# Long convolution of a decoder layer: blocks of 64 tokens on partition halves in place of blocks of 128

## Chip, cores and metric

The kernel runs on one core of a Trainium2 chip. The metric is device time in microseconds. Before the change three runs took 2181.34, 2184.97 and 2187.56 us; their median is 2184.97 us. All data are float32.

The engines are called PE (TensorE, matrix multiply), DVE (VectorE), ACT (ScalarE), POOL (GpSimd) and SP (SyncE, which here only issues transfers). A PE matmul needs a weight load ahead of it, shown as PEld.

## What is computed

A decoder layer on x of 16 sequences x 512 tokens x 256 channels: a gated long-convolution block, then self plus cross attention, then a low-rank feed-forward, each followed by a layer norm. The change touches the first part:

```python
z = rmsnorm(u, pre_norm_w) @ in_proj_w.T              # 768 channels
z_pre = conv1d(z, short_w, causal, 3 taps, per channel) + short_b
x2, x1, v = split(z_pre, 3)
h = sum_s residues[:, s] * exp(log_poles[:, s] * t)   # a filter of 512 taps per channel, 16 poles
xv = x1 * v
y = (causal_convolution(xv, h) + xv * D_skip) * x2
y = y @ out_proj_w.T + u                              # then an MLP
```

## The kernel before

**Two parts, each with its own plan.** The front (until about 326 us) works out the long convolution of all sequences; its results go to DRAM. The loop then takes one sequence after another through the gate, the MLP, attention and the feed-forward. In each part the operations are first collected (`plan.op`: engines, a cost, a function, a priority, what it reads and writes) and then ordered by the class `Plan` (lines 62 to 195): a list scheduler in which each engine takes the startable operation of lowest priority number. Each operation's tiles come from named pools and are bound in that planned order. Engines and transfer queues then work in that order, each waiting where its input is not there. `Plan.change` (line 96) adds a bonus to a PE operation that has the same array tiling as the one before, with the constants `HOLD` and `STAY`.

**Projection** (`project(b)`, line 422, once a sequence). x is loaded; `rms_ops` squares it on ACT; `rsqrt_op` works out the factor on POOL; `scale_ops` (line 325) scales the four row blocks of 128 x 256 on DVE (line 330); PE transposes (line 344); six matmul groups (line 456) give the 768 channels; ACT (line 463) and DVE (line 471) apply the three taps; POOL multiplies x1 by v (line 487); PE transposes the product (line 495), and it is kept as `xv`: 128 token positions on the partitions, and per channel 4 blocks x 16 sequences. The gate x2 goes to DRAM (line 481). Weights of the loop are loaded in between; POOL scales two of them (line 787).

**Long convolution** (lines 582 to 708), in blocks of 32 channels, eight in all. Time is cut into 4 blocks of 128 tokens:
- *toe*: within a block of tokens the filter is a 128x128 Toeplitz matrix per channel. It is read from `hpad` in DRAM with overlapping rows (`load_toe`, line 593: 8 channels, 512 KB, 32 loads in all); POOL clears the part beyond the diagonal (line 602); `toe_mm` (line 670) multiplies, two channels at once on the two column halves of the array.
- *near*: `near_mm` (line 619) reduces a block of tokens to 16 states per channel, four channels at once on column groups of 32; DVE moves the result out (line 629).
- *recurrence*: two steps per channel block carry the states from one token block to the next (POOL, lines 639 and 647), through one tile `tmp`.
- *far*: ACT evaluates exponentials (line 655); `far_mm` (line 683) adds the older blocks' share to toe's result in PSUM.
- ACT and DVE copy the sums to `row` tiles (line 694, by the helper at lines 297 and 299), and ACT issues the writes to `yconv` in DRAM (line 701, 64 of 128 KB).

**Hand-over to the loop.** SP issues the loads of `yt` from `yconv` (`load_y`, line 1002, two per sequence), of the gate (line 1008) and of x (line 1011); POOL multiplies y by the gate (line 1020); PE begins with the output projection (line 1033).

Before, `toes`, `far`, and the x tiles share the pool "x" of 11 tiles; the pool "row" has 9.

## Time and profile before

| What | Value |
|---|---|
| Median of three runs | 2184.97 us |
| Profiled execution | 2186.31 us, span 2184.6 us |
| Instructions in the span | 35354 |
| PE busy | 2037.0 us (93%) |
| DVE busy | 1361.0 us (62%) |
| ACT busy | 943.6 us (43%) |
| POOL busy | 663.5 us (30%) |
| Granted PE clock | 0.97 |
| Transfers | 177.94 MB, mean 81 GB/s |

The profile is one execution. In its groups a row gives line, engine, operation, output <- input by tile names (`fmm`, `mm` are PSUM tiles, `fx` a tile of the pool "x", `frow` one of "row"), shapes, count, and in the timeline the start and the length of the stretch; the bracket at its end gives the idle time before it and what ended that. "issue" means that the engine waited for nothing that the profile shows. In the names of array tiles, 128*64 is 128 rows by 64 columns.

The front's stages are seen by the lines that run in them: projection (line 456 on PE) from 11.4 to 228 us, near, toe and far (lines 619, 670, 683) from 229.0 to 308.5 us, and the first output projection (line 1033) at 326.4 us.

### The profile page before, as it was taken

The numbers are of one execution on the slowest core, as the hardware profiler recorded it, in microseconds if no ns is written. First come the engines' busy times: TensorE is split into PE (matmuls) and PEld (weight loads), VectorE is DVE, ScalarE is ACT, GpSimd is POOL, SyncE is SP. The second block draws the span as 40 slices with busy tenths as digits, with TensorE's granted clock in tenths as the row PEclk, the third lists the DMA queues.
The fourth block names the chain that finished last, engine by engine and source line by source line (L and its number), as shares of the span: only waits on it lengthen the run. The fifth ranks groups of instructions, "written<-read, shape, count | busy, mean of one in ns | idle before, by whom it ended". The sixth has DMA issues, their size and how long they took to land.

```text
span 2184.6 us, 35354 instructions
## 1 busy us (share of the span) xinstructions
PE 2037.0 (93%) x14324; PEld 1053.6 (48%) x14324; DVE 1361.0 (62%) x1988; ACT 943.6 (43%) x1385; POOL 663.5 (30%) x896
## 2 busy tenths in 40 slices
PE   8999758979899999999999999999999999999676
PEld 4444545535454545454545454545454545454332
DVE  7988311746565757575757575757575757575642
ACT  7765312142526262626262626262626262625243
POOL 3333451131323232324232424242424242323222
PEclk9999978989999999999999999999999999999888
DMA  5342582122222222222232313131313131212200
GB/s 176 123 133 83 198 270 73 49 63 66 70 59 89 59 88 61 83 66 86 62 91 57 94 55 93 56 94 55 95 54 96 52 87 52 68 51 68 61 11 10
DMA packets 113733, 177.94 MB, mean 81 GB/s; under 512 B 13217, under 2 KB 61858, under 8 KB 113442
## 3 DMA queue, kind: packets, MB, share of 16 engines
q1 hardware_dynamic: 108450, 167.29, 25.0%
q10 hardware_dynamic: 5120, 8.39, 1.2%
q8 instruction: 112, 1.84, 0.3%
q14 instruction: 51, 0.42, 0.1%
HBM read 109.00 MB, written 66.67 MB: 80 GB/s over the span
## 4 chain that ended last, share of the span: by engine, by line
PE 84%; ACT 5%; DVE 5%; DMA 3%; issue 2%; POOL 1%; ACTq 0%; SPq 0%; POOLq 0%; DVEq 0%
PE mm L1058 13%; PE scores L1302 10%; PE mm L1211 8%; PE mm L1110 7%; PE scores L1380 7%; PE av L1415 7%; PE fmm L456 6%; PE mm L1605 4%; PE av L1621 3%; PE mm L1139 3%; PE mm L972 2%; DMA fx<-hpad 2%; PE mm L344 2%; PE mm L1467 2%; ACT ex L1392 2%
## 5 line engine op out<-in xcount | busy, mean ns | idle before, releaser
L1392 ACT ACTIVATE ex<-scores 128x2048 f32<-128x2048 f32 x160 | 300.1, 1876 | 176.7 <-PE scores L1380 174.0
L1058 PE MATMUL mm<-xT,w_l 128*128 128x512 f32 x640 | 296.0, 606 | 0.0
L1403 POOL TENSOR_SCALAR_AFFINE_SELECT ex<-ex 128x512 f32<-128x512 f32 x256 | 158.0, 635 | 382.4 <-ACT ex L1392 351.1
L1302 PE MATMUL scores<-keys,q 32*128 32x320 f32 (+4 forms) x2560 | 233.8, 472 | 42.8 <-DVE maxes L1332 18.3
L1321 DVE TENSOR_TENSOR scores<-scores,mask_qk 128x512 f32<-128x512 f32 (+1 forms) x192 | 168.3, 876 | 101.9 <-PE scores L1302 97.9
L1302 PEld LDWEIGHTS scores<-keys,q 32*128 32x128 f32 x2560 | 116.5, 190 | 179.0 <-issue 57.8
L1613 ACT ACTIVATE row<-mm,b_s 128x512 f32<-128x512 f32 x128 | 80.8, 684 | 253.6 <-PE mm L1605 253.4
L1380 PE MATMUL scores<-q,keys 32*128 32x512 f32 (+3 forms) x2048 | 183.1, 460 | 7.1 <-ACT ex L1392 7.0
L1058 PEld LDWEIGHTS mm<-xT,w_l 128*128 128x128 f32 x640 | 115.6, 190 | 145.9 <-issue 128.6
L456 PE MATMUL fmm<-fx,inw 128*128 128x512 f32 x384 | 177.2, 607 | 2.2 <-ACT fx L299 2.2
L957 ACT ACTIVATE xt<-xt,small 128x256 f32<-128x256 f32 x192 | 102.7, 595 | 173.7 <-POOL small L950 173.7
L1549 POOL TENSOR_TENSOR nd<-nd,nd 128x1024 f32<-128x1024 f32 x30 | 70.6, 2354 | 347.3 <-DMA nd<-di 347.3
L1415 PE MATMUL av<-ex,va 128*32 128x512 f32 (+3 forms) x2048 | 168.1, 439 | 0.0
L306 POOL TENSOR_SCALAR small<-small 128x4 f32<-128x4 f32 (+1 forms) x66 | 13.1, 199 | 509.6 <-DVE small L942 508.1
L1070 ACT ACTIVATE row<-mm 128x512 f32<-128x512 f32 x80 | 47.8, 597 | 271.0 <-PE mm L1058 271.0
L297 DVE COPY row<-av 128x512 f32<-128x512 f32 x66 | 45.7, 692 | 184.0 <-PE av L1415 165.5
L1110 PE MATMUL mm<-w_l,gT 128*128 128x256 f32 x640 | 158.9, 384 | 0.0
L471 DVE SCALAR_TENSOR_TENSOR frow<-fmm,cw,frow 128x511 f32<-128x511 f32 x192 | 140.2, 745 | 14.5 <-ACT frow L463 10.5
L1334 DVE TENSOR_REDUCE maxes<-scores 128x4 f32<-128x2048 f32 x64 | 146.7, 2293 | 2.2
L1380 PEld LDWEIGHTS scores<-q,keys 32*128 32x128 f32 x2048 | 89.3, 183 | 104.4 <-ACT ex L1392 33.8
L1110 PEld LDWEIGHTS mm<-w_l,gT 128*128 128x128 f32 x640 | 117.9, 190 | 43.8 <-issue 30.3
L1217 DVE TENSOR_SCALAR q<-mm,bqc_s 128x512 f32<-128x512 f32 x63 | 47.3, 751 | 140.0 <-PE mm L1211 140.0
(177 smaller groups left out, 3322.8 us busy)
## 6 DMA issues: line engine op xcount, KB each, us to landing
dn<-row SPq DMA_DIRECT2D x120, 256.0 KB
fx<-hpad SPq DMA_DIRECT2D x32, 512.0 KB
keys<-dk SPq DMA_DIRECT2D x64, 256.0 KB
nd<-dn SPq DMA_DIRECT2D x30, 512.0 KB
nd<-di SPq DMA_DIRECT2D x30, 512.0 KB
fx<-in_x SPq DMA_DIRECT2D x16, 512.0 KB
gates<-frow SPq DMA_DIRECT2D x32, 256.0 KB
yconv<-frow ACTq DMA_DIRECT2D x64, 128.0 KB
```

Of the source, the lines that this page charges most:

```text
L456: nc.tensor.matmul(ps.t, inw[:, k, bass.ts(m, P)], xT.t[:, k, :], start=(k == 0), stop=(k == KD - 1))
L471: lambda e, m=m, lag=lag, ps=ps, t=t: nc.vector.scalar_tensor_tensor(t.t[:, lag:], ps.t[:, 0 : T - lag], cw[:, m, 2 - lag : 3 - lag], t.t[ ...
L1058: nc.tensor.matmul(ps.t, w[:, k, bass.ts(f, P)], zT.t[:, k, :], start=(k == 0), stop=(k == KD - 1))
L1110: nc.tensor.matmul(ps.t[:, bass.ts(cc, D)], gT.t[:, f, bass.ts(c, P)] if f < NF else gE.t, w_l3[:, f, :] if f < NF else w_l3e[:, c, :], st ...
L1211: nc.tensor.matmul(ps.t, w[:, k, cols], xT.t[:, k, :], start=(k == 0), stop=(k == KD - 1))
L1302: nc.tensor.matmul(sc.t[:, r, at : at + hi - lo], q.t[hd, bass.ts(i, P)], kk.t[hd, lo:hi], start=True, stop=True,)
L1321: nc.vector.tensor_tensor(diag, diag, mask, ALU.add)
L1334: nc.vector.tensor_reduce(own[:, 3], sc.t, AX.X, ALU.max, negate=True)
L1380: nc.tensor.matmul(sc.t[:, r, at : at + T - j * P], keys[g].t[hd, TC + j * P : TC + (j + 1) * P], qas[g].t[hd, j * P :], start=True, stop= ...
L1392: lambda e, sc=sc, ex=ex: nc.scalar.activation(ex.t.rearrange("p (r n) -> p r n", r=HPG), sc.t, AF.Exp, scale=scale),
L1403: lambda e, ex=ex, at=at: nc.gpsimd.affine_select(out=ex.t.rearrange("p (r n) -> p r n", r=HPG)[:, :, at : at + P], in_=ex.t.rearrange("p ...
L1415: nc.tensor.matmul(av[g].t[bass.ts(r, SLOT), j * P :], va.t[:, j, h * VS : h * VS + SLOT], ex.t[:, r * T + at : r * T + at + n], start=(j ...
```

## The change

The token blocks of the long convolution become 64 long, so there are eight instead of four. The two blocks of a pair lie on the two partition halves that they already have in `xv`.

- The Toeplitz matrices are 64x64. A load covers 16 channels and fills both partition halves with the same values by two transfers of 256 KB; there are 16 such tiles in place of 32. POOL clears them by a multiplication with a constant triangle `tri` instead of a select. `toe_mm` uses array tiles of 64x64, four at once.
- `near_mm` uses tiles of 64x32 and works out both halves separately, into two PSUM tiles; two evictions on DVE. `far_mm` runs per half, 64 columns each.
- The recurrence has six steps in place of two; a step (two instructions) may go to DVE or to POOL, as the planner chooses.
- `far` has a pool of its own (2 tiles); "x" has 10 tiles, "row" 8. The state tile is twice as wide.
- `yconv` gets a leading index for the half; `load_y` issues four loads per sequence in pieces of 256 bytes in place of two in pieces of 512.
- In the front, x is scaled on POOL; the projection matmuls are only planned once their `row` tile is free (`holds`); the planner's tiling bonus is 0 in the front and 1000 in the loop as before.

```diff
-    def __init__(self, tiles):
+    def __init__(self, tiles, hold=0, stay=0):
         self.tiles, self.ops = tiles, []
+        self.HOLD, self.STAY = hold, stay
...
-    HOLD, STAY = 1000, 1000
...
-    hpad = dram.tile([D + 1, P], F32, name="hpad")
-    yconv = dram.tile([NT, B, D, P], F32, name="yconv")
+    HB = P // 2
+    hpad = dram.tile([D + 1, HB], F32, name="hpad")
+    yconv = dram.tile([2, NT, B, D, HB], F32, name="yconv")
...
-    def scale_ops(x, sq, prio, on="DVE"):
+    def scale_ops(x, sq, prio, on):
         for c in range(NT):
             def fn(e, c=c):
-                if e == "DVE":
-                    nc.vector.tensor_scalar(x.t[:, c, :], x.t[:, c, :], sq.t[:, c, 8:9], None, ALU.mult)
+                if e == "POOL":
+                    nc.gpsimd.tensor_scalar(x.t[:, c, :], x.t[:, c, :], sq.t[:, c, 8:9], None, ALU.mult)
                 else:
                     nc.scalar.activation(x.t[:, c, :], x.t[:, c, :], AF.Copy, scale=sq.t[:, c, 8:9])
-            plan.op(on, 0.4 if on == "DVE" else act(D, True), fn, prio, r=[sq], w=[(x, c)])
+            plan.op(on, pool_(D) if on == "POOL" else act(D, True), fn, prio, r=[sq], w=[(x, c)])
...
-            "x": tiles(fp_, "fx", 11, [P, R8 * P]),
-            "row": tiles(fp_, "frow", 9, [P, T]),
-            "state": tiles(fp_, "state", 2, [P, R8, HPG * B]),
+            "x": tiles(fp_, "fx", 10, [P, R8 * P]),
+            "row": tiles(fp_, "frow", 8, [P, T]),
+            "state": tiles(fp_, "state", 2, [P, R8, 2 * NT * B]),
+            "far": tiles(fp_, "far", 2, [P, R8, HB]),
...
+        tri = fp_.tile([P, HB], F32, name="tri")
+        nc.gpsimd.memset(tri, 1.0)
+        for n in range(2):
+            half = bass.ts(n, HB)
+            nc.gpsimd.affine_select(
+                out=tri[half, :], in_=tri[half, :], compare_op=ALU.is_ge, fill=0.0, base=HB - 1,
+                pattern=[[-1, HB]], channel_multiplier=-1,
+            )
...
-            scale_ops(x_, sq, pr - 120)
+            scale_ops(x_, sq, pr - 120, "POOL")
...
-                plan.op("PE", KD * pe(T), mm, pr + 10, r=[xT, INW], w=[ps])
+                plan.op("PE", KD * pe(T), mm, pr + 10, r=[xT, INW], w=[ps], holds=[t])
...
-            for c in range(HPG):
-                toe = View("x", lambda t: t.rearrange("p (d u) -> p d u", u=P))
-                def load_toe(e, toe=toe, at=d0 + c * R8):
-                    hp = hpad[at : at + R8, :]
-                    src = bass.AP(hp.tensor, hp.offset, [[1, P], [1, R8 * P]])
-                    nc.sync.dma_start(out=toe.t.rearrange("p d u -> p (d u)"), in_=src)
-                early = blk * HPG + c < 5
+            for cp in range(HPG // 2):
+                toe = View("x", lambda t: t.rearrange("p (d u) -> p d u", u=HB))
+                def load_toe(e, toe=toe, at=d0 + cp * 2 * R8):
+                    hp = hpad[at : at + 2 * R8, :]
+                    for n in range(2):
+                        src = bass.AP(hp.tensor, hp.offset, [[1, HB], [1, 2 * R8 * HB]])
+                        nc.sync.dma_start(out=toe.t[bass.ts(n, HB)].rearrange("p d u -> p (d u)"), in_=src)
+                early = blk * HPG // 2 + cp < 5
                 plan.op(
-                    "SP", 0.4, load_toe, pc - 50, r=[HPAD], w=[toe], lat=4.0,
-                    after=at_seq(4 + c if early else B - 1),
+                    "SP", 1.0, load_toe, pc - 50, r=[HPAD], w=[toe], lat=4.0,
+                    after=at_seq(4 + 2 * (blk * HPG // 2 + cp) if early else B - 1),
                 )
                 plan.op(
-                    "POOL", 1.35,
-                    lambda e, toe=toe: nc.gpsimd.affine_select(
-                        out=toe.t, in_=toe.t, compare_op=ALU.is_ge, fill=0.0, base=P - 1,
-                        pattern=[[0, R8], [-1, P]], channel_multiplier=-1,
+                    "POOL", pool_(2 * R8 * HB),
+                    lambda e, toe=toe: nc.gpsimd.tensor_tensor(
+                        toe.t, toe.t, tri.unsqueeze(1).to_broadcast([P, 2 * R8, HB]), ALU.mult
                     ),
                     pc - 50, w=[toe],
                 )
                 toes.append(toe)
-            ps, st = Buf("mm"), Buf("state")
-            far = View("x", lambda t: t.rearrange("p (r u) -> p r u", u=P))
+            pss, st = [Buf("mm"), Buf("mm")], Buf("state")
+            far = Buf("far")
             for rr in range(0, R8, 2):
-                def near_mm(e, rr=rr, ps=ps, d0=d0):
+                def near_mm(e, rr=rr, pss=pss, d0=d0):
                     for r in range(rr, rr + 2):
                         for c in range(HPG):
                             d = d0 + c * R8 + r
-                            nc.tensor.matmul(
-                                ps.t[bass.ts(c, SLOT), bass.ts(r, (NT - 1) * B)],
-                                near[:, d * NS : d * NS + SLOT], xv[:, d, 0 : (NT - 1) * B],
-                                start=True, stop=True,
-                            )
-                plan.op("PE", 0.25, near_mm, pc, r=[XV, NEAR], w=[ps], tiling=COLS4)
-            def evac_state(e, ps=ps, st=st, blk=blk):
-                n = (NT - 1) * B
-                nc.vector.tensor_tensor(
-                    st.t[:, :, B:], ps.t[:, 0 : R8 * n].rearrange("p (r n) -> p r n", n=n),
-                    rsT[:, bass.ts(blk, R8)].unsqueeze(2).to_broadcast([P, R8, n]), ALU.mult,
-                )
-            plan.op("DVE", 0.6, evac_state, pc, r=[ps, (LP, "T1")], w=[st])
-            for j in range(2, NT):
+                            for n in range(2):
+                                half = bass.ts(n, HB)
+                                nc.tensor.matmul(
+                                    pss[n].t[bass.ts(c, SLOT), bass.ts(r, NT * B)],
+                                    near[half, d * NS : d * NS + SLOT], xv[half, d, :], start=True, stop=True,
+                                )
+                plan.op("PE", 0.45, near_mm, pc, r=[XV, NEAR], w=pss, tiling=BOTH, holds=[st])
+            for n in range(2):
+                def evac_state(e, n=n, ps=pss[n], st=st, blk=blk):
+                    cols = (NT - n) * B
+                    at = NT * B if n == 0 else B
+                    nc.vector.tensor_tensor(
+                        st.t[:, :, at : at + cols], ps.t.rearrange("p (r n) -> p r n", r=R8)[:, :, 0:cols],
+                        rsT[:, bass.ts(blk, R8)].unsqueeze(2).to_broadcast([P, R8, cols]), ALU.mult,
+                    )
+                plan.op("DVE", 0.7, evac_state, pc, r=[pss[n], (LP, "T1")], w=[(st, n)])
+            for j in range(2, 2 * NT):
+                before, at = ((j - 1) % 2 * NT + (j - 1) // 2) * B, (j % 2 * NT + j // 2) * B
+                def step(e, before=before, at=at, st=st, blk=blk, tmp=None):
+                    eng = nc.vector if e == "DVE" else nc.gpsimd
+                    eng.tensor_tensor(
+                        tmp.t, st.t[:, :, before : before + B],
+                        aT[:, bass.ts(blk, R8)].unsqueeze(2).to_broadcast([P, R8, B]), ALU.mult,
+                    )
+                    eng.tensor_tensor(st.t[:, :, at : at + B], st.t[:, :, at : at + B], tmp.t, ALU.add)
                 tmp = Buf("tmp")
                 plan.op(
-                    "POOL", 0.5,
-                    lambda e, j=j, tmp=tmp, st=st, blk=blk: nc.gpsimd.tensor_tensor(
-                        tmp.t, st.t[:, :, bass.ts(j - 1, B)],
-                        aT[:, bass.ts(blk, R8)].unsqueeze(2).to_broadcast([P, R8, B]), ALU.mult,
-                    ),
-                    pc, r=[st, (NEAR, "a")], w=[tmp],
-                )
-                plan.op(
-                    "POOL", 0.5,
-                    lambda e, j=j, tmp=tmp, st=st: nc.gpsimd.tensor_tensor(
-                        st.t[:, :, bass.ts(j, B)], st.t[:, :, bass.ts(j, B)], tmp.t, ALU.add
-                    ),
-                    pc, r=[tmp], w=[st],
+                    "DVE POOL", (0.6, 1.0), lambda e, step=step, tmp=tmp: step(e, tmp=tmp), pc,
+                    r=[(NEAR, "a")], w=[st, tmp],
                 )
             for r in range(R8):
...
+            for cp in range(HPG // 2):
+                def toe_mm(e, cp=cp, ys=ys, toe=toes[cp], d0=d0):
+                    for r in range(R8):
+                        for cc in range(2):
+                            c = 2 * cp + cc
+                            for n in range(2):
+                                half = bass.ts(n, HB)
+                                nc.tensor.matmul(
+                                    ys[c].t[bass.ts(n ^ cc, HB), bass.ts(r, HB)], xv[half, d0 + c * R8 + r, :],
+                                    toe.t[half, cc * R8 + r, :], start=(r == 0), stop=False,
+                                    skip_group_check=True,
+                                )
+                plan.op("PE", 1.2, toe_mm, pc + 10, r=[XV, toes[cp]], w=ys[2 * cp : 2 * cp + 2], tiling=(HB, HB))
+            for rr in range(0, R8, R8 // 2):
+                def far_mm(e, rr=rr, ys=ys, st=st, far=far):
+                    for r in range(rr, rr + R8 // 2):
+                        for n in range(2):
+                            for c in range(HPG):
+                                part = slice(c * SLOT, c * SLOT + NS)
+                                nc.tensor.matmul(
+                                    ys[c].t[bass.ts(n ^ c % 2, HB), bass.ts(r, HB)],
+                                    st.t[part, r, bass.ts(n, NT * B)], far.t[part, r, :],
+                                    start=False, stop=True, skip_group_check=True,
+                                )
+                plan.op("PE", 0.95, far_mm, pc + 10, r=[st, far], w=ys, tiling=(SLOT, P // 2))
             for c in range(HPG):
-                def toe_mm(e, c=c, ys=ys, toe=toes[c], d0=d0):
-                    for rp in range(R8 // 2):
-                        for par in range(2):
-                            r = par * R8 // 2 + rp
-                            nc.tensor.matmul(
-                                ys[c].t[bass.ts(par, 64), bass.ts(rp, P)], xv[:, d0 + c * R8 + r, :],
-                                toe.t[:, r, :], start=(rp == 0), stop=False, skip_group_check=True,
-                            )
-                plan.op("PE", 0.9, toe_mm, pc + 10, r=[XV, toes[c]], w=[ys[c]], tiling=COLS2)
-            for par in range(2):
-                def far_mm(e, par=par, ys=ys, st=st, far=far):
-                    for rp in range(R8 // 2):
-                        r = par * R8 // 2 + rp
-                        for c in range(HPG):
-                            part = slice(c * SLOT, c * SLOT + NS)
-                            nc.tensor.matmul(
-                                ys[c].t[bass.ts(par, 64), bass.ts(rp, P)], st.t[part, r, :], far.t[part, r, :],
-                                start=False, stop=True, skip_group_check=True,
-                            )
-                plan.op("PE", 0.65, far_mm, pc + 10, r=[st, far], w=ys, tiling=(SLOT, P // 2))
...
-                        lambda e, c=c, o=o, par=par, d0=d0: nc.scalar.dma_start(
-                            out=yconv.rearrange("j b d t -> (j b) d t")[
-                                :, d0 + c * R8 + par * R8 // 2 : d0 + c * R8 + (par + 1) * R8 // 2, :
+                        lambda e, c=c, o=o, n=n, d0=d0: nc.scalar.dma_start(
+                            out=yconv[n].rearrange("j b d t -> (j b) d t")[
+                                :, d0 + c * R8 : d0 + (c + 1) * R8, :
                             ],
-                            in_=o.t[bass.ts(par, 64)],
+                            in_=o.t[bass.ts(n ^ c % 2, HB)],
...
-    plan = Plan(pool)
+    plan = Plan(pool, 1000, 1000)
...
         def load_y(e, k):
-            nc.sync.dma_start(
-                out=yt.t[:, k, :].rearrange("p (j t) -> p j t", j=NT),
-                in_=yconv[:, b, bass.ts(k, P), :].rearrange("j p t -> p j t"),
-            )
+            for n in range(2):
+                nc.sync.dma_start(
+                    out=yt.t[:, k, :].rearrange("p (j n t) -> p j n t", n=2, t=HB)[:, :, n],
+                    in_=yconv[n, :, b, bass.ts(k, P), :].rearrange("j p t -> p j t"),
+                )
...
-            plan.op("SP", 0.1, lambda e, k=k: load_y(e, k), p0 - 500, w=[(yt, k)], lat=4.0)
+            plan.op("SP", 1.0, lambda e, k=k: load_y(e, k), p0 - 500, w=[(yt, k)], lat=4.0)
```

## The prediction

> **What bounds the kernel now.** I read the windows first, to find the stage that the change touches; then PE's timeline inside it, for what ends its waits; then the DMA queues; last the chain behind it. Columns of the windows: length, then busy time and count for PE, weight loads (PEld), DVE, ACT, POOL, then granted clock, DMA share, GB/s.
>
> ```profile
> core 0: us, PE busy (x) PEld busy (x) DVE busy (x) ACT busy (x) POOL busy (x), PEclk, DMA share, GB/s
> 200.00:220.00 20.00, 19.69 (x66) 10.02 (x65) 18.03 (x31) 11.54 (x15) 5.17 (x6) 1.00 0.25 64
> 240.00:260.00 20.00, 12.86 (x288) 11.34 (x286) 3.51 (x6) 6.65 (x21) 8.45 (x11) 0.95 0.73 255
> 280.00:300.00 20.00, 15.69 (x281) 14.18 (x279) 3.50 (x6) 2.34 (x4) 14.62 (x21) 0.79 0.92 352
> ...
> 1000.00:1200.00 200.00, 199.33 (x1410) 100.22 (x1408) 125.75 (x173) 89.74 (x114) 64.23 (x82) 1.00 0.27 81
> ```
>
> Up to 229 us (projection) PE is full. From 229.0 to 308.5 us (the convolution, 79.5 us) no engine is full, but the DMA engines are at 0.9: 27 of the 32 Toeplitz loads of 512 KB fall here. From about 400 us the loop keeps PE at 99.7%. In the built programs PE, DVE, ACT and POOL hold the same loop instructions in the same order before and after, so only the front (0 to 326 us) can move the time, if the loop's loads stay hidden.
>
> The Toeplitz load is halved, so the question is what bounds the convolution next. PE's timeline at its start, before the loads collect:
>
> ```profile
> 229.03 1.90 PE L619 MATMUL fmm<-xv,near 128*32 128x48 f32 x157
> 234.88 2.72 PE L619 MATMUL fmm<-xv,near 128*32 128x48 f32 x128 [3.95 <-issue]
> 238.60 1.30 PE L619 MATMUL fmm<-xv,near 128*32 128x48 f32 x99 [1.01 <-issue]
> 239.83 1.85 PE L670 MATMUL fmm<-fx,xv 128*64 128x128 f32 x29
> 242.61 2.18 PE L670 MATMUL fmm<-fx,xv 128*64 128x128 f32 x35 [0.92 <-issue]
> ```
>
> PE stops with nothing to wait for ("issue"), after 128 records, and again after 99 + 29 = 128. Each matmul record has a weight load beside it, so a stop comes every 256 instructions. The page says what that is:
>
> ```profile
> PE 2037.0 (93%) x14324; PEld 1053.6 (48%) x14324; DVE 1361.0 (62%) x1988; ACT 943.6 (43%) x1385; POOL 663.5 (30%) x896
> ...
> q8 instruction: 112, 1.84, 0.3%
> ```
>
> 2 x 14,324 instructions over 112 packets is 256 per packet, 1.84 MB / 112 = 16.4 KB: PE fetches its code in pages of 256 instructions, and small matmuls use up a page faster than the next arrives. The DMA view of 238 to 242 us, with one stop in it, has nothing else on the engines:
>
> ```profile
> DMA packets 1, 0.02 MB, mean 4 GB/s; under 512 B 0, under 2 KB 0, under 8 KB 0
> q8 instruction: 1, 0.02, 1.4%
> ```
>
> From page to page: 238.60 - 234.88 = 3.72 us, 242.61 - 238.60 = 4.01 us; mean **3.87 us**. In it the packet starts 1.0 to 1.6 us after the page begins (235.92, 240.15 us in the trace) and lasts 1.0; PE goes on some 1.6 us later. Under the full DMA of 248 to 303 us the packet starts 0.6 to 7.9 us after its page, mean 4.7.
>
> **The change, part by part.**
>
> *Convolution, PE.* near, toe and far each go from 256 to 512 matmuls. A float32 matmul leaves two records with two weight loads (512 records for 256 matmuls on L619, L670, L683). So 3 x 256 x 4 = 3,072 PE instructions become 6,144: 12 pages become 24. Streams alone shrink: toe runs at 55 ns a record (32 in 1.97 us, two tiles at once) and far at 22; halved columns on four or eight tiles should give some 14 and 11; with near at 11, 1,024 x (11 + 14 + 11) ns = 37 us, 1.4 to 1.8 us a page, far below 3.87. So pages set the pace. The 57 instructions to the next page boundary take 0.3 us; the first page lasts 5.5 us (229.33 to 234.88 before; its successor's packet was late behind Toeplitz and gate transfers, and such stand there again); then 22 pages at c, and 1.7 us of work in the last: 7.5 + 22c. For c the ends are 3.5 (the shortest such step in the convolution, 267.71 to 271.21) and 5.1. DMA work left is 6 loads x 128 packets x 180 ns and the yconv writes (1.2% of 16 engines' span, 419 engine-us): (138 + 419)/16 = 35 us of about 100, a share of 0.34; between 1.27 us of start delay at none and 4.7 at 0.9 a straight line gives 2.55, so c = 3.87 + 1.28 = 5.1. A queue grows slower than a line at first, so I take **c = 4.3**: 102.1 us. Against 79.5: **+22.6** (ends +5 and +40).
>
> [...]
>
> [...] The new toe_mm sends both row halves of a channel group into one bank. No row of before does this. Unhindered 14 ns a record; serial 53 (half of 107, twice the 55 above, for half the columns): 6.8 us a page, 2.5 over c on 8 pages, +20. I take nothing, since even two at once (27 ns, 3.4 us) stays under c; the 20 goes into the range.
>
> *Convolution, the rest, hidden under 3c = 12.9 us a block.* Two masks on POOL as multiply, 2.35 us each for 1,024 elements (L1549) instead of four selects of 1.09: 4.7. Six recurrence steps instead of two, serial through one tmp tile, 0.40 + 0.46 + 0.1 us each on POOL at most (L639, L647): 5.8. ACT: 8 DMA issues of 0.55, 2 copies of 0.58, 8 exponentials of 64 columns of 0.24 (L580): 7.5. DVE: two evictions of 0.6, two copies of 0.69, some steps: about 5. Late next if cover is gone: the last far, two pages (8.6 us) after the last near; its eviction and steps take 7.0. Nothing added.
>
> *Projection.* Scaling x moves to POOL. One 256-column row there: L787 takes 1.97 us for 672, L306 0.20 for 4, so 0.87 us; four 3.5 against 1.14 on DVE. The first sequence has no cover: **+2.4**. Later ones are a sequence ahead (13.4 us each; POOL then has 1.25 + 3.5 + 2.5 = 7.3). A gain is in reach here:
>
> ```profile
> 160.63 7.94 POOL L787 TENSOR_SCALAR w_l<-w_l,postw 128x672 f32<-128x672 f32 x4 [1.83 <-DMA postw<-in_post_w]
> ```
>
> ```profile
> 175.84 0.36 PE L344 MATMUL fmm<-ident,fx 128*128 128x128 f32 x1 [3.35 <-issue]
> 176.94 3.56 PE L344 MATMUL fmm<-ident,fx 128*128 128x128 f32 x15 [0.74 <-DVE fx L330]
> ```
>
> The weight scaling held up POOL's rsqrt, PE ran dry for 4.3 us and restarted at a clock of 0.80 to 0.86, some 2.5 more. In the changed order one x more is scaled ahead of it, and about 18 us of PE work cover its 13: **-7** (ends 0 and -10: all visible PE gaps of the projection are some 22 us, most with other causes). Fewer row tiles (8) and the hold on them: 0 to +6, taken 0; waits for rows now are under 5 us in all (ACT L463 behind DVE L471). Sum **-4.5**.
>
> *Hand-over.* Last far to first loop matmul now:
>
> ```profile
> 317.43 3.15 DMA yconv<-frow
> 320.64 0.37 SPq L1002
> 321.06 3.87 DMA gate<-gates
> 325.06 1.27 POOL yt L1020
> ```
>
> The last write is issued 9.5 us after the last far, as ACT still has a block of writes before it (6 us of issues and copies against 5.1 between the last two fars). With blocks 12.9 us apart only its own 6.2 remain: -3.3. One more load stands before the gate, 0.37, and 1,024 pieces of 256 B for 512 of 512 B, at most 30 ns each over 16 engines: +0.3 more likely than +1. **-2.6**. In the loop the two extra loads per sequence (0.7 us of SP in 107) lie beside a full PE: 0.
>
> *Sum*: -4.5 + 22.6 - 2.6 = +15.5. The profiled execution took 2186.3 (span 2184.6 and 1.7 around it), giving 2201.8; it lies 1.3 above the median 2185.0: **2201 us**.
>
> **Rivals.**
> (a) *Pages cost nothing in time*, and the halved transfers count. For: DMA is at 0.9 now, and many pages of the busy stretch passed with no stop. Against: those lasted 6 us and more. Then ACT is next: 8 x 7.5 + 7 lead-in = 67, -12.5; projection -4.5; ACT's backlog at the end stays: about 2169, faster. It decides if a page comes in under 2.5 us.
> (b) *Fetching at its quickest*, c = 3.5 to 3.7, and a projection gain near -8: +5 to +9, -8, -2.6, no change: 2182. For: 3.50 was seen under a loaded DMA.
> (c) *Fetches queue, or the toe banks collide*: c = 5.1, or 2.5 us on 8 pages: +40 or +43, less 7: 2219. For: the delays of 3 to 8 us in the busy stage.
> (d) *POOL becomes late in the projection*, eating the -7 and some: +8 on the forecast, 2209; inside the forecast's range.
>
> **How the numbers follow.** Chances: forecast with (d) 0.58, (a) 0.13, (b) 0.12, (c) 0.17. A measurement tells 0.3% (6.5 us) from no change. Faster is (a) and a little of (b): 0.14; same is the rest of (b) and the low edge of the forecast: 0.14; slower 0.72. Range: below 2181 lies most of (a), above 2232 a tail of (c); the forecast's own range is 2190 to 2214.
>
> **What would show it.** Right: code packets double by 12 (112 to 124); in the convolution PE stops on "issue" every 128 records; page to page about 4.3 us; DMA share near 0.35 there; last far near 326 us; no PE gap behind the weight scaling. Wrong: a convolution under 80 us, or PE waiting there for POOL, DVE or loads instead of issue; toe records 50 ns apart.

## Result: 0.33% slower, about half of what was forecast

After the change five runs have a median of 2192.95 us (2190.96 to 2194.23); five runs of the kernel before lie at 2184.97 (2181.34 to 2189.62). The ratio is 1.0033, with an interval of 1.0017 to 1.0049. The forecast was 2201 with a range of 2181 to 2232: the sign is right, the size is not (+8 measured, +16 forecast). The two profiled executions differ by 4.7 us (2190.96 and 2186.31; spans 2189.25 and 2184.59); by them the difference can be followed stage by stage:

| Stage, us | before | after | difference | forecast |
|---|---|---|---|---|
| first near matmul (end of the projection) | 229.03 | 218.34 | -10.7 | -4.5 |
| convolution, first near to last far | 79.47 | 94.53 | +15.1 | +22.6 |
| last far to first output projection | 17.87 | 16.39 | -1.5 | -2.6 |
| from there to the first transposes of y | 9.33 | 11.41 | +2.1 | 0 |
| rest of the loop | 1848.9 | 1848.6 | -0.3 | 0 |
| sum | 2184.6 | 2189.3 | +4.7 | +15.5 |

The windows of the kernel after, with the columns of the windows shown before (length, busy time and count of PE, weight loads, DVE, ACT, POOL; granted PE clock, DMA share, GB/s):

```profile
200.00:220.00 20.00, 20.00 (x191) 10.17 (x193) 17.86 (x24) 9.85 (x13) 14.39 (x8) 1.00 0.47 125
240.00:260.00 20.00, 13.32 (x559) 11.70 (x559) 11.44 (x24) 5.94 (x19) 9.91 (x8) 0.50 0.60 157
280.00:300.00 20.00, 14.26 (x749) 12.96 (x748) 8.33 (x23) 6.38 (x20) 3.41 (x8) 0.74 0.44 102
1000.00:1200.00 200.00, 199.34 (x1410) 99.03 (x1410) 125.18 (x176) 92.70 (x120) 65.87 (x86) 1.00 0.27 81
```

From 280 to 300 us, in the convolution, the DMA share fell from 0.92 to 0.44, yet PE is no fuller: it is busy for 14.3 of 20 us, with 749 matmul records where it had 281. Its clock is lower as well (0.50 and 0.74 in the two windows of the stage). PE's timeline at the start of the stage shows what stops it:

```profile
218.34 1.57 PE L637 MATMUL fmm<-xv,near 64*32 64x64 f32 x128
219.84 0.58 PE L692 MATMUL fmm<-fx,xv 64*64 64x64 f32 x24
223.02 2.18 PE L692 MATMUL fmm<-fx,xv 64*64 64x64 f32 x104 [2.60 <-issue]
225.13 0.64 PE L637 MATMUL fmm<-xv,near 64*32 64x64 f32 x23
226.63 1.78 PE L637 MATMUL fmm<-xv,near 64*32 64x64 f32 x105 [0.85 <-issue]
228.34 0.91 PE L692 MATMUL fmm<-fx,xv 64*64 64x64 f32 x23
232.28 3.06 PE L692 MATMUL fmm<-fx,xv 64*64 64x64 f32 x105 [3.02 <-issue]
```

Between two stops lie 104 + 23 = 127 and 105 + 23 = 128 records, so 256 instructions with the weight loads. PE stops in this way at 19 of the 23 page boundaries of the stage, and each of the 19 stops ends 1.2 to 1.6 us after a packet of code has come in (worked out from the transfer records). The long stop that ends at 232.28 us is one of them: its packet starts at 229.47, 2.8 us after its page, and lasts 1.3. The counts of the whole run show the code too:

```profile
PE 2040.0 (93%) x15860; PEld 1058.1 (48%) x15860; DVE 1375.1 (63%) x2002; ACT 938.2 (43%) x1385; POOL 722.1 (33%) x942
...
q8 instruction: 124, 2.03, 0.4%
```

That is 1,536 more matmul records, as many more weight loads, and 12 more packets (124 for 112). And the groups of PE from 218 to 313 us, with what ended its idle time:

```profile
L692 PE MATMUL fmm<-fx,xv 64*64 64x64 f32 x1024 | 30.3, 289 | 17.2 <-issue 17.2
L706 PE MATMUL fmm<-far,state 16*64 16x64 f32 x1024 | 19.6, 301 | 7.2 <-issue 6.8 <-ACT frow L300 0.4
L637 PE MATMUL fmm<-xv,near 64*32 64x64 f32 x1024 | 17.7, 291 | 4.5 <-issue 4.0 <-ACT frow L300 0.5
```

28.0 us of idle time end on "issue", 0.9 on data. From 223.02 to 310.82 us the trace has 22 pages, so a page takes 87.8 / 22 = **3.99 us**.

A later part of PE's timeline shows a boundary without a stop, and how much the granted clock does:

```profile
284.44 1.05 PE L706 MATMUL fmm<-far,state 16*64 16x64 f32 x45 [1.33 <-issue]
285.42 1.99 PE L692 MATMUL fmm<-fx,xv 64*64 64x64 f32 x64
287.34 2.09 PE L637 MATMUL fmm<-xv,near 64*32 64x64 f32 x128
289.36 0.56 PE L692 MATMUL fmm<-fx,xv 64*64 64x64 f32 x18
291.60 0.92 PE L692 MATMUL fmm<-fx,xv 64*64 64x64 f32 x46 [1.68 <-issue]
292.45 1.14 PE L706 MATMUL fmm<-far,state 16*64 16x64 f32 x82
...
303.26 1.56 PE L692 MATMUL fmm<-fx,xv 64*64 64x64 f32 x47 [2.71 <-issue]
304.75 1.56 PE L706 MATMUL fmm<-far,state 16*64 16x64 f32 x81
```

From 284.44 us PE runs 45 + 64 + 128 + 18 = 255 records, two pages, without stopping between them: at half the clock the matmuls of the first of them last 3.3 us, and its packet is in at 286.53 us, 1.2 us before the boundary at 287.74. So the work of a page can last about as long as its fetch. The granted clock was 1.00 from 288.97 to 295.79 us and 0.50 from 302.62 on. 46 records of toe take 0.92 us in the first stretch and 47 take 1.56 in the second; 82 of far take 1.14, and 81 take 1.56. The pages do not follow the clock: in ten runs with all the matmuls (the kernel after, e2 to e5, e7 and e10 to e13 below, 22 pages each) the mean page is 4.06 us in the 142 pages wholly at half the clock and 4.13 in the 9 wholly at full clock, at a DMA share of 0.41 and 0.43. So the fetch sets the page's length in the main, and not the matmuls in it.

### The profile page after: what moved, and what is told of

It reads as the page before. It is cut to its first block, busy times and chain, and to the rows that moved or that the text cites. A ratio compares the mean times of both kernels' runs of the same rounds, so it can differ in the third digit from the quotient of the medians.

```text
span 2189.3 us, 38505 instructions
## 1 busy us (share of the span) xinstructions
PE 2040.0 (93%) x15860; PEld 1058.1 (48%) x15860; DVE 1375.1 (63%) x2002; ACT 938.2 (43%) x1385; POOL 722.1 (33%) x942
## 4 chain that ended last, share of the span: by engine, by line
PE 84%; ACT 5%; DVE 5%; issue 2%; POOL 2%; DMA 2%; ACTq 0%; SPq 0%; POOLq 0%; DVEq 0%
PE mm L1083 13%; PE scores L1327 10%; PE mm L1236 8%; PE mm L1135 7%; PE scores L1405 7%; PE av L1440 7%; PE fmm L471 5%; PE mm L1630 4%; PE av L1646 3%; PE mm L1164 3%; PE mm L996 2%; PE mm L345 2%; PE mm L1492 2%; ACT ex L1417 2%; PE scores L1466 2%
```

## Experiments

Convolution stage and pages of each run that bears on them. The mean page leaves out each run's first one and goes up to its last boundary; stream is PE's busy time in the stage divided by the pages. The front of e7 (below) has the same instructions in the same order on PE, DVE, ACT and POOL as the kernel after: 94.5 against 99.1 us is how far two executions of one front can lie apart. The runs e5, e10, e12 and e13, which have the same convolution too, took 95.8 to 99.3 us, with mean pages of 4.05 to 4.21. Each of e1 to e4, e11 and e12 was timed once.

| Run | convolution, us | pages | mean page, us | stream a page, us | DMA share |
|---|---|---|---|---|---|
| after | 94.5 | 24 | 3.99 | 2.73 | 0.49 |
| e7, the same front | 99.1 | 24 | 4.16 | 2.83 | 0.46 |
| e1, one half of far | 85.3 | 20 | 4.24 | 3.05 | 0.52 |
| e2, far half as wide | 95.9 | 24 | 4.04 | 2.62 | 0.48 |
| e3, 11 load tiles out | 89.9 | 24 | 3.81 | 2.70 | 0.36 |
| e4, loads twice | 103.3 | 24 | 4.37 | 2.85 | 0.56 |
| e11, tiling rule | 95.1 | 24 | 4.01 | 2.68 | 0.48 |

### Is it code, or the matmuls themselves? (e1, e2)

e1: one of the two halves in `far_mm` is left out, 1,024 PE instructions fewer, four pages.

```diff
-                        for n in range(2):
+                        for n in range(1):
```

> The changed kernel without the far matmuls of the first half's successor (256 of 512 left out, so half the token blocks lack the older blocks' share): 1,024 PE instructions fewer, four pages of 256. Theory of the code pages: the convolution (first near to last far, 94.5 us in the changed kernel) becomes 4 x 3.99 = 16 us shorter, about 78.5 us, and PE still stops on issue every 128 records. Rival, that the matmul streams and the waits around them set the pace: 512 records less at 13 to 17 ns, 7 to 9 us shorter, about 86 us.

e2: the same instructions, but each far matmul has 32 columns in place of 64.

```diff
-                                    ys[c].t[bass.ts(n ^ c % 2, HB), bass.ts(r, HB)],
-                                    st.t[part, r, bass.ts(n, NT * B)], far.t[part, r, :],
+                                    ys[c].t[bass.ts(n ^ c % 2, HB), r * HB : r * HB + HB // 2],
+                                    st.t[part, r, bass.ts(n, NT * B)], far.t[part, r, 0 : HB // 2],
```

> The changed kernel with every far matmul on 32 columns instead of 64 (half of far's contribution is left out), the same number of PE instructions. Theory of the code pages: the convolution stays at 94.5 us, within 2 us. Rival of the streams: far's 1,024 records of about 16 ns take half, 8 us less, about 86 us.

Measured: e1 took 2181.16 us (before beside it: 2188.09), its convolution 85.3, 9.3 less than in the kernel after. That is the figure of the rival (about 86), not the 78.5 of the pages. e2 took 2189.89, its convolution 95.9, 1.3 more, which is inside the scatter. So fewer instructions help and fewer columns don't. But the two runs together also say that the stream is not what I took it for. First e2's timeline, then e1's, one stretch of far each, both at half the clock:

```profile
259.60 1.51 PE L706 MATMUL fmm<-far,state 16*64 16x32 f32 x85
```

```profile
258.57 1.98 PE L706 MATMUL fmm<-far,state 16*64 16x64 f32 x64
```

With half the columns a record takes 1.51 us / 85 = 18 ns; in the kernel after far takes 1.56 / 81 = 19 ns at the same clock. Something other than columns sets most of that pace, so e2 left the stream nearly as it was and cannot speak against it. In e1, with only one half's four array tiles in turn, a record takes 31 ns. So e1 removed 512 records but made the other far records slower: the stream of a page rose from 2.73 to 3.05 us, and 6 of its 18 full pages end without a stop, after 3.35 to 4.26 us of work. The four pages did go, but the remaining ones took 4.24 us in place of 3.99, which leaves 9.3 us and not 16. The slower stream is part of that; how much of it is scatter (4.16 in e7) the single run doesn't show. In e1, too, almost all of PE's idle time in the stage ends on issue (23.6 us). What tells pages from streams is therefore less e1 than the stops that end with the packets, and the pages that keep their length at either clock.

### What do transfers add to a page? (e3, e4)

e3: the Toeplitz loads are left out except for the five early tiles, 11 tiles of 512 KB.

```diff
+                if not early:
+                    load_toe = lambda e: None
```

> The changed kernel without 11 of its 16 Toeplitz loads (those after the first five tiles; the tiles keep older data). Theory that a code page is late because its packet stands behind data transfers: the step from page to page falls from 3.99 us to between 3.5 and 3.87, the long ones (5.65, 5.10, 6.12 us in the first half) go, and the convolution takes 84 to 92 us instead of 94.5. Rival, that the step does not depend on other transfers: 94 to 95 us. Rival, that the convolution waits for the loads themselves: over 10 us shorter, with no stops on issue left.

e4: every half of a Toeplitz tile is loaded twice.

```diff
-                    for n in range(2):
+                    for n in (0, 1, 0, 1):
```

> The changed kernel with each Toeplitz load issued twice (the same values into the same tile). Theory that transfers delay the code pages: the step from page to page rises from 3.99 us to 4.3 to 5.1, the convolution takes 101 to 119 us. Rival, that the step does not depend on other transfers: 94 to 97 us.

Measured: e3 took 2186.48 us and e4 2219.08. The windows of the stage, e3 and then e4:

```profile
218.30:308.16 89.86, 64.68 (x3073) 57.06 (x3072) 44.71 (x104) 21.98 (x64) 29.36 (x37) 0.66 0.36 86
```

```profile
239.24:342.49 103.25, 68.47 (x3073) 60.50 (x3072) 42.74 (x102) 22.19 (x64) 29.95 (x39) 0.58 0.56 146
```

Transfers do slow the pages: 3.81, 3.99 (4.16 in e7) and 4.37 us at a DMA share of 0.36, 0.49 (0.46) and 0.56. Both ends lie outside the scatter. The pages themselves say the same: sorted by the DMA share in each, the 220 pages of the ten runs take 3.67 us below 0.3 (84 pages), 3.99 from 0.3 to 0.45 (39), 4.35 from 0.45 to 0.6 (25) and 4.51 above (72). But the effect is small: a straight line through them rises by 1.7 us from a share of 0 to 1, where the prediction's rises by 3.8. At 0.49 the line of the prediction (1.27 us of delay at none, 4.7 at 0.9) would have given 1.27 + 0.49 x 3.8 = 3.1, and a page of 3.87 + 1.9 = 5.7. Only the long pages go in e3: none is over 4.8 us, while the kernel after has three of 5.1 to 6.1. Much of e4's loss is elsewhere: its projection ends 20.9 us later, with single waits of PE of up to 9.6 us for POOL's product (line 502). POOL works in its planned order, and there it stands at masks (line 618) whose Toeplitz loads are late, 25.1 us in all until the projection's end.

The DMA share had been forecast at 0.35. What it is without the late loads, the transfer view of e3 shows (the queue q10 carries ACT's writes to `yconv`):

```profile
q10 hardware_dynamic: 4166, 6.84, 32.8%
q8 instruction: 24, 0.39, 2.0%
```

So the writes alone hold 0.328 x 89.9 us x 16 engines = 472 engine-us (419 taken in the prediction), and the loads left in the stage of the kernel after about (0.49 x 94.5 - 0.36 x 89.9) x 16 = 220 (138 taken, for six loads; seven are issued from 217.8 us on).

### What shortened the projection? (e5, e6, e8, e9, e10, e13)

Two edits of the projection were set apart: scaling on POOL, and the hold on row tiles. Each was undone in the kernel after and put alone into the kernel before.

e5, in the kernel after, and e6, the other way round in the kernel before (of both edits only the call is shown; the helper `scale_ops` changes with it):

```diff
-            scale_ops(x_, sq, pr - 120, "POOL")
+            scale_ops(x_, sq, pr - 120, "DVE")
```

> The changed kernel with x scaled on DVE again. Theory that the move to POOL is what shortened the projection (first near at 218.3 us instead of 229.0): first near at 225 to 229 us, total 5 to 10 us over the changed kernel. Rival, that the hold on the row tile, the smaller filter and the new order did it: first near at 216 to 219 us, total 0 to 3 us under the changed kernel.

> The kernel before with x scaled on POOL and nothing else changed. Theory that the move to POOL shortens the projection: first near at 218 to 223 us, total 5 to 10 us under the kernel before (ratio 0.995 to 0.998). Rival: first near at 228 to 233 us, total 0 to 4 us over it.

e8, the kernel before with e6's edit and the hold; e9, the kernel before with the hold alone; e10, the kernel after without it:

```diff
-                plan.op("PE", KD * pe(T), mm, pr + 10, r=[xT, INW], w=[ps])
+                plan.op("PE", KD * pe(T), mm, pr + 10, r=[xT, INW], w=[ps], holds=[t])
```

> The kernel before with x scaled on POOL and with the projection matmuls planned only once their row tile is free. If both parts help the projection, first near at 216 to 219 us as in the changed kernel and a total 10 to 12 us under the kernel before; if the hold does nothing, the same as with the scaling alone within 1 us.

> The kernel before with one part of the change alone: the projection matmuls are planned only once their row tile is free (holds); x is still scaled on DVE. If the hold is what shortened the projection (the pair of runs with and without it, both with scaling on POOL, lay 8.9 us apart at the first near matmul), the first near comes at 229.0 - 8.9 = 220 us or earlier and the time falls to about 2175 us; if DVE scaling is also the better one with the hold, as it was in the kernel after (5.6 us), the first near comes at 208 to 213 us and the time is 2163 to 2169. If the hold is worth something only together with POOL scaling: first near at 229, 2185 us.

> The kernel after without the hold on row tiles in the projection. If the hold made the projection short there too: first near matmul at 218.3 + 9 = 227 us, time about 2202 us, and PE gaps behind the ctx load and row tiles come back. If another part did it (fewer Toeplitz loads in the plan, 8 row tiles): first near at 218, time 2193.

e13, the edits of e5 and e10 together, so that the blocks of 64 are left, with their pools and loads, the planner's tiling bonus of 0 and the higher cost of a y load:

> The kernel after with both edits of the projection undone: x scaled on DVE, no hold on row tiles. What is left of the change is the convolution in blocks of 64 with its pools and loads. With that convolution each edit undone alone had brought the first near matmul from 218.3 to 212.6. If the edits get in each other's way and each alone is a gain, as in the kernel before, the first near comes later again, at 218 to 229 us, with PE gaps behind the ctx load, and the time is 2193 to 2203 us. If the new convolution's own plan (fewer Toeplitz loads, pools) is what shortened the projection and either edit is a loss, the first near comes at 207 to 212.6 us and the time is 2182 to 2188.

Measured, with PE's idle and busy time from its first matmul to the first near (worked out from the matmul records):

| Convolution | scaling | hold | run | first near | PE idle | PE busy | median, us | ratio to before |
|---|---|---|---|---|---|---|---|---|
| 128 | DVE | no | before | 229.0 | 12.3 | 207.3 | 2184.97 | |
| 128 | POOL | no | e6 | 222.5 | 8.4 | 204.4 | 2179.52 | 0.9975 (0.9965 to 0.9984) |
| 128 | DVE | yes | e9 | 221.3 | 8.0 | 203.2 | 2176.94 | 0.9966 (0.9953 to 0.9979) |
| 128 | POOL | yes | e8 | 213.5 | 4.4 | 199.2 | 2169.90 | 0.9933 (0.9918 to 0.9948) |
| 64 | DVE | no | e13 | 214.6 | 4.4 | 200.6 | 2191.37 | 1.0029 (1.0016 to 1.0041) |
| 64 | POOL | no | e10 | 212.5 | 3.2 | 199.6 | 2187.32 | 1.0013 (1.0006 to 1.0020) |
| 64 | DVE | yes | e5 | 212.7 | 3.1 | 200.3 | 2190.32 | 1.0027 (1.0018 to 1.0037) |
| 64 | POOL | yes | after | 218.3 | 7.3 | 201.3 | 2192.95 | 1.0033 (1.0017 to 1.0049) |

Only e6 came as expected, and e9 nearly. e5 and e10 lie below both of their expected values for the first near, e8 gains more than it should, and e13 falls between its two cases.

Three things follow. What is left in e13 brings the first near forward by 14.4 us: the long gaps are gone. That was in neither term of my sum. Which part does it, the new order, the fewer Toeplitz loads or the pools, was not taken apart. By time e13 still loses 0.29%, since its convolution takes 99.3 us. Each edit alone brings the first near forward on either convolution, by 6.5 and 7.7 us in the kernel before and by 2 with blocks of 64, and both together by 15.5 in the kernel before; but with blocks of 64 both together lose 3.7 us against neither. And gaps can cost more than their length: from before to e8 the idle time falls by 7.9 us and the busy time of the same matmuls by another 8.2. Of this, 4.7 us lie in two stretches of the kernel before in which the granted clock is halved (66.7 to 70.1 and 175.9 to 182.8 us); e8 has no such stretch in its projection. Where the other 3.5 lie was not taken apart. Two places where the gaps were, before and then after:

```profile
150.00:156.00 6.00, 3.22 (x15) 1.96 (x15) 3.70 (x6) 2.76 (x9) 1.26 (x1) 1.00 0.54 182
170.00:190.00 20.00, 15.91 (x48) 8.79 (x47) 14.44 (x24) 7.43 (x16) 6.09 (x7) 0.83 0.34 92
```

```profile
150.00:156.00 6.00, 6.00 (x19) 2.86 (x18) 5.24 (x7) 4.62 (x13) 3.37 (x3) 1.00 0.22 72
170.00:190.00 20.00, 20.00 (x65) 9.99 (x64) 17.91 (x25) 9.20 (x14) 11.24 (x11) 1.00 0.36 90
```

Around the restart at 176 us PE does 48 records in 20 us at a clock of 0.83; undisturbed it does 65 at 1.00. The gap here is 3.35 + 0.74 us long, and the granted clock is 0.50 from 175.9 to 182.8 us. The length of a gap alone doesn't tell what follows: 2.12 us without work, ending at 52.2 us in the kernel after, were followed by 3.4 us at half the clock (53.4 to 56.9 us), while the 2.78 us for the ctx load in the kernel before, in the row from 150 us, were not (1.00). That gap has gone too.

Why both edits together lose with blocks of 64: POOL's timeline in the kernel after, then PE's line that waits for it.

```profile
121.13 1.27 POOL L502 TENSOR_TENSOR frow<-frow,frow 128x512 f32<-128x512 f32 x1
122.38 3.63 POOL L331 TENSOR_SCALAR fx<-fx,fsmall 128x256 f32<-128x256 f32 x4
126.10 0.20 POOL L307 TENSOR_SCALAR fsmall<-fsmall 128x4 f32<-128x4 f32 x1
126.38 1.04 POOL L308 TENSOR_TENSOR fsmall<-fsmall,mhalf 128x4 f32<-128x4 f32 x1
127.52 2.73 POOL L331 TENSOR_SCALAR fx<-fx,fsmall 128x256 f32<-128x256 f32 x3
130.21 1.27 POOL L502 TENSOR_TENSOR frow<-frow,frow 128x512 f32<-128x512 f32 x1
```

```profile
131.53 0.66 PE L510 MATMUL fmm<-ident,frow 128*128 128x128 f32 x4 [1.44 <-POOL frow L502]
```

The product x1 by v (line 502) stands behind scalings, and PE's transposes wait for it. Five such waits make up 6.0 us in the kernel after; they come to about 2.3 in e5 and 1.7 in e10. With the half-clock stretch behind the longest of them, 1.7 us more, that is about the 5.8 us between e10 and the kernel after. Why the planner puts them in that order only when both edits are there was not followed further.

### Order in the convolution and at its end (e11, e7, e12)

e11: the tiling bonus back in the front.

```diff
-        plan = Plan(pool)
+        plan = Plan(pool, 1000, 1000)
```

> The kernel after with the planner's tiling bonus of 1000 in the front as before; the same instructions, and on PE only the order of near, toe and far differs. If code pages set the pace, the order is of no account: convolution 94.5 us within 2, pages of 4.0, first near at 218.3, span 2189. If switches between array tilings cost time, the stage gets shorter by 3 us or more; if the rule makes PE wait for data, longer by 3 or more, with the waits on DVE, ACT or POOL instead of issue.

Measured: 2192.48 us, first near 218.8, convolution 95.1, pages 4.01: within the scatter of the kernel after. The order of near, toe and far doesn't show while pages set the pace, and nor does the tiling rule in this kernel.

e7: the planner's cost of a y load back from 1.0 to 0.1; e12: the four writes of constants before the loop (`dk`) issued by ACT in place of SP.

```diff
-            plan.op("SP", 1.0, lambda e, k=k: load_y(e, k), p0 - 500, w=[(yt, k)], lat=4.0)
+            plan.op("SP", 0.1, lambda e, k=k: load_y(e, k), p0 - 500, w=[(yt, k)], lat=4.0)
```

> The changed kernel with the planner's cost of a y load back at 0.1, which puts the first x load back ahead of the four key-row writes on SP. Theory: the first transposes of y in the loop start some 2 us earlier after the first output projection (9.3 us as before, instead of 11.4), total 2 us less. Rival: the x load is late for another reason, no change.

```diff
-            nc.sync.dma_start(out=t[bass.ts(par, HPG), HD:, :], in_=fixed[0 : HPG * HD, :])
+            nc.scalar.dma_start(out=t[bass.ts(par, HPG), HD:, :], in_=fixed[0 : HPG * HD, :])
```

> The kernel after with the four writes of constants (dk) issued by ACT in place of SP, so that nothing stands ahead of the first x load of the loop on SP. If these four issues are what made x late: x is issued 4 to 5 us sooner after the gate load, the first transposes of y come 9.3 us after the first output projection as in the kernel before (11.4 in the kernel after), span 2187. If not: 11.4 and 2189.

What they ask: after the hand-over the first addition of x to the output projection is late. SP's timeline of the kernel before, that of the kernel after, and DVE's lines, before and then after:

```profile
321.06 0.50 SPq L1008 DMA_DIRECT2D gate<-gates  x1
321.66 0.38 SPq L1011 DMA_DIRECT2D xt<-in_x  x1
322.09 2.49 SPq L924 DMA_DIRECT2D dk<-row  x4
324.62 6.39 SPq L1011 DMA_DIRECT2D xt<-in_x  x4
```

```profile
323.84 0.46 SPq L1033 DMA_DIRECT2D gate<-gates  x1
324.35 2.67 SPq L948 DMA_DIRECT2D dk<-row  x4
327.06 7.09 SPq L1036 DMA_DIRECT2D xt<-in_x  x5
```

```profile
330.39 0.69 DVE L983 TENSOR_TENSOR y<-mm,xt 128x512 f32<-128x512 f32 x1 [8.85 <-PE mm L1033]
```

```profile
335.41 1.29 DVE L1007 TENSOR_TENSOR y<-mm,xt 128x512 f32<-128x512 f32 x2 [18.26 <-DMA xt<-in_x]
```

The first x load, which stood ahead of the `dk` writes, now stands behind them, and DVE waits for it; in the kernel before DVE waited for PE there.

Measured: e7 took 2193.67 us (ratio 1.0043, 1.0028 to 1.0058) and left SP's order here as it was, so the load's cost in the plan is not the reason; what is stays open. In e12 (2193.05 us) x is issued at 0.52 us after the gate load instead of 3.22, and DVE no longer waits for x. From the first output projection to the transposes it takes 10.0 us (11.4 in the kernel after, 9.3 before, and 9.3 expected). But nothing is gained in all, since POOL's product of y and gate is late in turn:

```profile
332.81 2.48 POOL L1045 TENSOR_TENSOR yt<-yt,gate 128x512 f32<-128x512 f32 x2 [13.81 <-DMA gate<-gates]
```

The gate load, issued at 325.33, is in after 7.5 us, where it took 4.1 in the kernel after (323.84 to 327.94). In e12 loads of x of 512 KB follow it directly, the first three of five issued before 330 us, in the kernel after the four writes of 128 KB. From the last far to the transposes it is 29.2 us in e12 and 27.8 in the kernel after. So the wait for x is about 1.4 of the 2.1 us, and with all the x loads ahead the stretch before it is 2.8 us longer (19.2 us from the last far to the first output projection, 16.4 in the kernel after); in the kernel before only one went ahead. That the x loads are what holds up the gate load is likely, but no run separates it from the `dk` writes, which e12 puts on another queue at the same time.

## Why the prediction was right and wrong

**Right: pages of code set the convolution's pace.** "So pages set the pace" holds: 124 packets, 28.0 us of idle time on issue against 0.9 for data, no gain from order that can be seen (e11), stops that end with a packet, and pages that don't follow the clock. Only the stop after every 128 records is too strong: at 4 of the 23 boundaries there is none. POOL, DVE and ACT had the room forecast; the masks take 2.38 us (2.35 taken). Rival (a), pages that cost nothing in time, did not come true on this stage; by it the time would have been about 2169.

**Wrong in size: c = 4.3.** The mechanism was right and the term 22c was too large. A page took 3.99 us (4.16 in e7, with the same front), which over 22 pages is 6.8 us less, and the first page took 4.5, not 5.5; with 0.4 more in the last page that is the overestimate of 7.5 us. By e7 alone it would be 3. The step that failed is the straight line from delay to DMA share, with the halfway value on it: at a share higher than forecast (0.49 for 0.34) the pages were faster than forecast. Both ends of the line were too high. The 3.87 at its foot is the mean of two pages, and in one of them the packet started 1.55 us after its page; in e3 the first three full pages, with almost nothing else on the DMA engines (a share of 0.02 to 0.03), take 3.61, 3.45 and 3.56. And the rise with the share is 1.7 us where 3.8 was taken. The reason given for the halfway value, a queue that grows slowly at first, doesn't show in any run: pages sorted by share rise evenly (3.67, 3.99, 4.35 and 4.51 us). The end of the range is too wide above: no mean page came near 5.1, even with the loads doubled (4.37). A small misreading had no effect: of the 27 Toeplitz loads said to fall into the convolution before, two were issued ahead of it, at 217.3 and 228.5 us.

**Wrong, without effect on the sum: the stream.** 14, 11 and 11 ns a record for toe, far and near had been taken, 1.4 to 1.8 us a page; the stage has 2.73. The prediction left out the clock. From the start of one record to that of the next it is 16, 11 and 11 ns where the granted clock is 1.00, close to what was taken, and 27, 16 and 15 where it is 0.50, which is most of the stage (0.62 on average). At the clock of this stage PE's work alone is 65.6 us, about the 67 of rival (a). Whether PE would have had a higher clock without its stops, no run shows.

**Right: no collision of toe's banks.** The +20 in the range stood for two row halves that hinder each other in one bank, and no run shows this term. At full clock toe's 16 ns lie well below the 53 estimated for a serial run and the 27 for two at once. At half the clock e1's far, four array tiles with a PSUM tile each, takes 27 ns from record to record, as toe does with two row halves in one PSUM tile.

**Wrong: the projection at -4.5.** It was -10.7. The startup cost was right (first matmul group of line 471 at 13.76 instead of 11.41 us: +2.35, 2.4 taken; a scaling 0.91 us, 0.87 taken), and so was the vanished gap behind the weight scaling. Failed has the assumption that "most with other causes" meant that the other gaps stay, so that everything but the two scaling terms was put at nothing: the gap for the ctx load and those around 62 us went as well, and the latter with a slow restart (a clock of 0.50 from 66.7 to 70.1 us). e13 shows how large this is: with neither edit of the projection in it the first near still comes 14.4 us sooner. Of the -10.7, 5.1 is idle time and 6.0 the same matmuls running faster, less a start 0.4 later. The hold, "taken 0", is a gain of 7.7 where it stands alone and a loss of 5.8 in this kernel. Rival (d), POOL late in the projection, is what the 6.0 us behind line 502 are, though it came with a gain and not instead of it.

**Hand-over: -1.5 for -2.6, and a load overlooked.** ACT ends the issue of the last write 8.2 us after the last far, where it was 9.5 before and 6.2 had been forecast. Two writes of the block before still stood ahead of its own, until 315.45 us. From the end of that issue to the first output projection it is 8.1 us (8.3 before), though two more y loads stand in SP's queue. The first x load, past which the `dk` writes moved, is the case of a queue whose order I did not list to its end: +2.1.

**Sum.** The spans differ by 4.7 where 15.5 was forecast: -7.5 convolution, -6.2 projection, +1.1 hand-over, +2.1 x load, -0.3 rest. The two large errors have the same sign, so they add up. The medians differ by 8.0, as the profiled execution of the kernel after lies 2.0 below its median and that of the one before 1.3 above.

## What to carry to other kernels

Count instructions, not columns, when matmuls get small: in this stage every 256 PE instructions cost a page of code of 3.8 to 4.4 us, and halving far's columns (e2, 4.04 us) or doubling the granted clock (4.13 against 4.06) hardly changed that, so doubling their number ate up the halved transfers. A gap in PE's work can cost more than its length, by the slower clock after it (in the two stretches at half the clock that e8 no longer has, 4.7 us of busy time); look for what any new order does to all gaps, not to the one that the edit aims at. And an edit to a planned order has no value of its own: by the first near the hold was worth -7.7 and -9.0 us with blocks of 128, -1.9 and +5.8 with blocks of 64. The best of the kernels here keeps blocks of 128 and takes the two small edits alone (e8): 2169.90 us, 0.67% below the kernel before and about 1% below the kernel after.

## What the hardware showed that was not expected

An instruction of the recurrence on DVE takes 0.29 us, but 2.34 to 2.40 where it starts just after POOL has begun to multiply a Toeplitz tile by the triangle. DVE's timeline of the kernel after, then POOL's:

```profile
229.57 2.38 DVE L660 TENSOR_TENSOR tmp<-state,aT 128x128 f32<-128x128 f32 x1
231.98 0.29 DVE L664 TENSOR_TENSOR state<-state,tmp 128x128 f32<-128x128 f32 x1
232.31 0.29 DVE L660 TENSOR_TENSOR tmp<-state,aT 128x128 f32<-128x128 f32 x1
232.63 2.35 DVE L664 TENSOR_TENSOR state<-state,tmp 128x128 f32<-128x128 f32 x1
```

```profile
229.46 2.34 POOL L618 TENSOR_TENSOR fx<-fx,tri 128x1024 f32<-128x1024 f32 x1 [1.71 <-DMA fx<-hpad]
232.46 2.37 POOL L618 TENSOR_TENSOR fx<-fx,tri 128x1024 f32<-128x1024 f32 x1 [0.66 <-DMA fx<-hpad]
```

Of these 72 instructions between 215 and 315 us, five take 2.34 to 2.40 us, and each of the five lies beside a run of line 618 and ends within 0.2 us of it; none of the other 67 runs inside one. In the rows above POOL is ahead by 0.11 and 0.17 us, in all five by 0.10 to 0.19. The four DVE instructions that start 0.01 to 0.22 us ahead of POOL's run and reach into it take 0.29 us. Why, the runs don't show; I had costed the steps without it. PE waits for DVE nowhere in this stage, so it cost nothing.

PE's granted clock fell to 0.62 over the convolution, as against 0.87 before, with PE busy for 69% of the stage (65.6 of 94.5 us) and 72% before (57.0 of 79.5), and the runs don't say why the one clock is so much lower than the other. It slows the records, as shown above, but most of what they lose lies under the fetch: pages wholly at half the clock take 4.06 us, wholly at full clock 4.13.
